# Splitting the last group of a decoder's last three layers into two sets of two batches

## The chip, the core and the metric

The kernel runs on one core of a Trainium2 chip. The metric is device microseconds of one execution. The profiler records one execution; all times inside the kernel come from that record, counted in microseconds from the start of its span. PE is the matrix engine, DVE the vector engine, ACT the scalar engine, POOL the general-purpose one, SP the engine that issues most DMAs.

## What is computed

A decoder of four blocks of three layers each runs over x, 32 batches of 128 tokens of width 128. Only the last block matters here:

```python
x = x + _L3_attn_ref(_layernorm(x), L3_attn_key_param, ...)   # layer 9
x = x + _L3_xattn_ref(_layernorm(x), ctx, ctx, mask, ...)     # layer 10
x = x + _L3_ffn_ref(_layernorm(x), weight_q, ...)             # layer 11
```

Layer 9 is an attention of 16 heads over 32 learned patterns whose weights are a sparsemax: the 32 scores of a token and head are sorted in descending order, the threshold tau is the largest of the means of the first k sorted scores less 1/k, and the weights are max(z - tau, 0). Layer 10 is a one-head attention over a context with a multiplicative mask. Layer 11 is a product with an integer weight: the normed row is scaled by its largest absolute value, clipped, rounded to whole numbers, multiplied, and scaled back.

## The kernel before

The 32 batches lie in 8 groups (G = 8) of 4 batches (J = 4); group i is the tile xg[i], 128 x 512 fp32. layer9() at its end writes out a schedule by hand for layers 9, 10 and 11 together. It is a loop over periods i = 0 to G + 2, each of 15 slots n = 0 to 14. In period i, slot n:

- sort(i, n) does step n of a merging sort of group i, for i below 8: two DVE tensor_tensor instructions (max and min) over up to 128 x 1024 elements each, and before them, where the step leaves elements untouched, two ACT copies of those. A step reads what the step before wrote, copies included.
- attend(i - 1) takes the sorted scores of the group before: slots 0 to 3 turn them over on PE, find tau, subtract it on POOL; slots 3 to 7 turn the weights over (turn_z), multiply with the values; slots 8 to 11 put the heads in order and project, and DVE adds the result to x.
- layer10(i - 2) does slots 0, 1, 2, 3, 5, 6, 7, and its first two steps (the norm) lie in slots 12 and 14 of the period before.
- scores(i + 1) makes the scores of the next group in slots 4, 6, 7, 8, 11, 12.
- layer11(i - 2) does slots 8, 10, 11, 12, 14 and its last step slot 0 of the next period.

follow(T, A, V) makes PE, ACT and DVE keep the order of this program while there are sorts; once slot == G * 15 the call follow() lifts that, and the tail (the attend, layer 10 and layer 11 of the last group) is ordered by the tool's own scheduler. POOL and SP are never held to it. In periods 0 to 2 pieces of layer 8 are mixed in.

Layer 11's rounding is a pair of tensor_scalar instructions on E, which is POOL but for the last group, where it is DVE (L2088 and L2089; adding and subtracting 1.5 * 2^23 leaves whole numbers). The second writes bf16. In slot 14 PE turns the bf16 tile over against a bf16 identity and ACT copies it out; in slot 0 of the next period PE multiplies with wq, DVE scales and adds (four scalar_tensor_tensor, one tensor_tensor) and SP sends x out (L2104).

```python
        E.tensor_scalar(q, q, 127.0, -128.0, ALU.min, ALU.max)      # L2088
        E.tensor_scalar(qb, q, rnd, rnd, ALU.add, ALU.subtract)     # L2089, qb is bf16
```

PSUM has three tags of two buffers each: ps (one bank a buffer), two and acc. Every turning over and most products take a ps; in layer 10 the tile of scores keeps one of the two ps buffers from slot 1, where it is written, to slot 3, where the last exp reads it.

SP's loads of context and mask for layer 10 (L325, L2027) are written in slot 12, but SP is not held to the program's order, so they run ahead.

Nearly all DVE, ACT and PE rows carry line L192, the helper that records the order; rows are told apart by their tiles. bbig holds sorted scores, gbig scores (z) and the re-ordered heads, xn a normed x, s small columns.

Of the kernel before, what the change touches and what calls it, by code (L numbers as in the profile page):

```python
# [10 lines left out]
F32 = mybir.dt.float32  # L11
# [191 lines left out]
def program(ctx, tc, cols, x, ctxt, mask, drop, dfirst, dsmall, dwide, drows, dunits, dexperts, dconst, drel, dwq, out):  # L203
# [38 lines left out]

    def follow(*engines):

        for e in (V, A, T):
            e.keep(e in engines)
# [107 lines left out]
    def norm_act(src, o):  # L354

        st, mv, rs, sh = small(J, 6), small(J, 2), small(J), small(J)
        for j in range(J):
            V.bn_stats(st[:, j, :], src[:, j, :])
        for j in range(J):
            V.bn_aggr(mv[:, j, :], st[:, j, :])  # L360
        V.tensor_scalar(rs, mv[:, :, 1], EPS, None, ALU.add)
        P.tensor_tensor(rs, rs, K["nhalf"], ALU.pow)
        yield
        V.scalar_tensor_tensor(sh, mv[:, :, 0], -1.0, rs, ALU.mult, ALU.mult)
        for j in range(J):
            A.activation(o[:, j, :], src[:, j, :], AF.Identity, bias=sh[:, j : j + 1], scale=rs[:, j : j + 1])
        yield

    def layernorm_act(i):

        xn = mid.tile([128, J, D], F32, tag="xn", name="xn", bufs=2)
        steps = norm_act(xg[i], xn)
        next(steps)
        yield
        next(steps)
        xnT = mid.tile([128, 512], F32, tag="xnT", name="xnT", bufs=2)
        transposed(xn, xnT, A.copy)
        yield xnT
# [1457 lines left out]
    def layer9():  # L1836
# [16 lines left out]
        def scores(i):  # L1853

            steps = norm_turned(i, WW["L3_attn_bo"])
            next(steps)
            yield
            next(steps)
            yield
            xnT = next(steps)  # L1860
            yield
            qT = linearT(W["a3_Wq"], xnT, W["L3_attn_bq"])
            z = zs[i] = gbig((128, J, 512))
            yield
            for part in range(2):
                p = two()
                for j in range(2):
                    at = (2 * part + j) * 128
                    mm(p[:, j], qT[:, at : at + 128], flat(kb))
                A.mul(z[:, 2 * part : 2 * part + 2], p, 8**-0.5)  # L1870
                ordered[i] = flat(z)
                yield
# [4 lines left out]
        def sort(i, n):  # L1877

            p, d = steps[n]
            cur, nxt = ordered[i], bbig()  # L1880
            ordered[i] = nxt
            a, b = (t.rearrange("p (n k) -> p n k", k=2 * p) for t in (cur, nxt))
            if d < p:
                A.copy(b[:, :, 0:d], a[:, :, 0:d])
                A.copy(b[:, :, 2 * p - d :], a[:, :, 2 * p - d :])
                a, b = (t[:, :, d : 2 * p - d] for t in (a, b))
            lo, hi, lo2, hi2 = (
                bass.AP(t.tensor, t.offset + at, [list(t.ap[0]), list(t.ap[1]), [2 * d, max(p // d - 1, 1)], [1, d]])
                for t in (a, b) for at in (0, d))
            V.tensor_tensor(lo2, lo, hi, ALU.max)  # L1890
            V.tensor_tensor(hi2, lo, hi, ALU.min)

        def attend(i):

            z, top, sTs, aTs = zs[i], ordered[i], {}, {}

            def turn_top(c):
                t = ps()
                for j in range(J):
                    T.transpose(t[:, j * 128 : (j + 1) * 128], top[:, j * 512 + c * 128 : j * 512 + c * 128 + 128], ident)  # L1900
                sTs[c] = bmid()
                A.activation(sTs[c], t, AF.Identity, bias=K["minus"])

            def lower(c):
                tau, m, sT = small(J, 4), acc((128, J, 4, 32)), sTs.pop(c)
                for j in range(J):
                    mm(m[:, j].rearrange("p h k -> p (h k)"), sT[:, j * 128 : (j + 1) * 128], K["means"])
                V.tensor_reduce(tau, m, AX.X, ALU.max)
                part = z[:, :, c * 128 : c * 128 + 128].rearrange("p j (h k) -> p j h k", k=32)
                P.tensor_tensor(part, part, bc(tau, 3, 32), ALU.subtract)  # L1910

            def turn_z(c):
                t = ps()
                for j in range(J):
                    T.transpose(t[:, j * 128 : (j + 1) * 128], z[:, j, c * 128 : (c + 1) * 128], ident)
                aTs[c] = bmid()
                A.activation(aTs[c], t, AF.Relu)
# [17 lines left out]
            yT_ps = acc()  # L1935
# [5 lines left out]
            yT = gmid()  # L1941
# [4 lines left out]
            rows = gbig((32, 16, 16, 8))  # L1946
            for c in range(0, 4, 2):
                t = two((32, 8, 128))
                for n in range(8):
                    T.transpose(t[:, n, :], by[:, 4 * c + n, :], ident)  # L1950
                A.copy(rows[:, :, 4 * c : 4 * c + 8, :], t.rearrange("p l (h e) -> p h l e", h=16))
                yield
            t = ps((128, 16, J, 8))
            for h in range(16):
                T.transpose(t[:, h].rearrange("p j l -> p (j l)"), rows[:, h].rearrange("p l e -> p (l e)"), ident[0:32, 0:32])
            yT = gmid((128, J, 16, 8))
            for j in range(J):
                A.copy(yT[:, j], t[:, :, j])
            yield
            zs.pop(i), ordered.pop(i)  # L1960
            project(i, yT.rearrange("p j h l -> p (j h l)"), W["a3_Wo"], None)
# [18 lines left out]
        for i in range(G + 3):  # L1980
            for n in range(15):
                todo = []
                add = lambda f, g, *at: todo.extend((f, g) for a in at if a == n and 0 <= g < G)
                add(layer11, i - 3, 0)
                add(attend, i - 1, 0, 1, 2, 3, 4, 5, 6, 7, 8, 9, 10, 11)
                add(layer10, i - 2, 0, 1, 2, 3, 5, 6, 7)
                add(layer10, i - 1, 12, 14)
                add(scores, i + 1, 4, 6, 7, 8, 11, 12)
                add(layer11, i - 2, 8, 10, 11, 12, 14)
                schedule.append((i, n, todo))  # L1990
        follow(T, A, V)
        for slot, (i, n, todo) in enumerate(schedule):
            if slot == G * 15:
                follow()
# [4 lines left out]
            if i < G:  # L1999
                sort(i, n)  # L2000
# [8 lines left out]

    def norm_turned(i, bo):  # L2010

        xn, xnT = (mid.tile(shape, F32, tag=tag, name=tag, bufs=2) for shape, tag in (([128, J, D], "xn"), ([128, 512], "xnT")))
        steps = norm_act(xg[i], xn)
        next(steps)
        yield
        next(steps)
        P.tensor_tensor(xg[i], xg[i], bc(bo, 1, J), ALU.add)
        yield
        transposed(xn, xnT, A.copy)
        yield xnT  # L2020


    def layer10(i):

        E = P if i < G - 1 else V
        c, dm = load_ctx(i), gmid((128, J, D))
        SY.dma_start(out=dm, in_=drop[i * J : i * J + J].rearrange("b q k -> q b k"))  # L2027
# [7 lines left out]
        s = ps((128, J, 128))  # L2035
        for j in range(J):
            cols_j = slice(j * 128, (j + 1) * 128)
            mm(s[:, j, :], xnT[:, cols_j], ctxT[i][:, cols_j])
        m, den, rec = small(J), small(J), small(J)
        pr = bmid((128, J, 128))  # L2040
# [3 lines left out]
        for half in range(2):  # L2044
            for j in (2 * half, 2 * half + 1):
# [5 lines left out]
        prT = bmid()  # L2051
        transposed(pr, prT, A.copy)
        yield
        o = ps()
        for j in range(J):
            cols_j = slice(j * 128, (j + 1) * 128)
            mm(o[:, cols_j], c[:, j, :], prT[:, cols_j])
        yT = gmid()
        A.copy(yT, o)
        yield  # L2060
        p = ps((128, J, 128))
        for j in range(J):
            mm(p[:, j, :], yT[:, j * 128 : (j + 1) * 128], W["x3_W"])
        for j in range(J):
            V.scalar_tensor_tensor(xg[i][:, j, :], p[:, j, :], rec[:, j : j + 1], xg[i][:, j, :], ALU.mult, ALU.add)
# [3 lines left out]
    def layer11(i):  # L2069

        rnd = 1.5 * 2.0**23
        E = P if i < G - 1 else V
        xn = mid.tile([128, J, D], F32, tag="xn", name="xn", bufs=2)
        steps = norm_act(xg[i], xn)
# [3 lines left out]
        P.tensor_tensor(xg[i], xg[i], bc(WW["qbias"], 1, J), ALU.add)  # L2078
        yield
        am, inv = small(J), small(J)  # L2080
# [4 lines left out]
        q, qb = bmid((128, J, D)), gmid((128, J, D), BF16)  # L2085
        for j in range(J):
            A.mul(q[:, j, :], xn[:, j, :], inv[:, j : j + 1])
        E.tensor_scalar(q, q, 127.0, -128.0, ALU.min, ALU.max)  # L2088
        E.tensor_scalar(qb, q, rnd, rnd, ALU.add, ALU.subtract)  # L2089
        yield  # L2090
        t = ps((128, 512), BF16)
        for j in range(J):
            T.transpose(t[:, j * 128 : (j + 1) * 128], qb[:, j, :], identb)
        qT = gmid((128, 512), BF16)
        A.copy(qT, t)
        yield
        p = ps((128, J, 128))
        o = bmid((128, J, D))
        for j in range(J):
            mm(p[:, j, :], qT[:, j * 128 : (j + 1) * 128], wq)  # L2100
        for j in range(J):
            V.scalar_tensor_tensor(o[:, j, :], p[:, j, :], am[:, j : j + 1], WW["qscale"], ALU.mult, ALU.mult)
        V.tensor_tensor(xg[i], xg[i], o, ALU.add)
        SY.dma_start(out=out[i * J : i * J + J].rearrange("b s d -> s b d"), in_=xg[i])  # L2104
# [53 lines left out]
```

## Time and profile before

| | us |
|---|---|
| median of 3 runs | 2979.89 (2970.95 to 2987.02) |
| the profiled execution | 2967.81, span 2965.9 |
| busy in the span: PE, DVE, ACT, POOL | 2552.0, 2072.2, 1504.4, 972.2 |
| the sorts' max and min, bbig from bbig, from 2400 us on | 237.4 in 224 instructions |
| L2089 (POOL, writes bf16) | 1.93 to 2.72, 7 times |
| L2104, x out: from issue to landing | 2.4 |

The periods can be read in the trace by the sort's first step, which reads gbig: it starts at 2758.5, 2806.3 and 2854.05. A full period is 47.75 us long; the last, with group 7's sort, 44.6 (to 2898.66); the tail 67.2. A row of the timeline gives start, duration, engine, line, operation, output and inputs, shapes, how many instructions were merged into it and, in brackets, how long the engine had been idle and what ended that. A row of the windows gives each engine's busy time and, after them, the granted clock of PE as a share of full speed.

### The profile page before, as it was taken

To read this page: it belongs to the slowest core of one execution; us is meant where nothing else is said; L and a number is where in the kernel's file an instruction comes from. 1 tells how busy PE (TensorE), PEld (TensorE's weight loads), DVE (VectorE), ACT (ScalarE), POOL (GpSimd) and SP (SyncE) were. 2 spreads that over 40 slices of the span, in tenths; PEclk is the share of its full clock that TensorE was granted. 3 is DMA by queue.
4 is the path that set the end of the run, shared out by engine and by line. 5 is a ranking of instruction groups with operands and counts; after the bars stand their busy time and mean duration, and the time that the engine had idled before them with its cause. 6 is when DMAs were issued, how large, how long until landed. Compare 5 with 4: busy or idle time off the path is not lost.

```text
span 2965.9 us, 55573 instructions
## 1 busy us (share of the span) xinstructions
PE 2552.0 (86%) x22609; PEld 1641.3 (55%) x22628; DVE 2072.2 (70%) x4121; ACT 1504.4 (51%) x3360; POOL 972.2 (33%) x1009
## 2 busy tenths in 40 slices
PE   6889999999889989999998999987886977976664
PEld 3555667777644446566664444445554666644443
DVE  6877667878878756677786544458886415789893
ACT  4555545444412256666664444457773323456663
POOL 4443342223210123334551000124442365324432
PEclk8877789999999999999999999989997998998786
DMA  3000000000000010000000000000002255210000
GB/s 113 2 2 2 6 20 8 5 8 1 12 11 1 0 33 2 5 9 9 12 2 15 1 1 0 1 1 2 2 2 82 94 179 166 91 29 12 22 11 18
DMA packets 50464, 73.44 MB, mean 25 GB/s; under 512 B 3841, under 2 KB 40962, under 8 KB 50082
## 3 DMA queue, kind: packets, MB, share of 16 engines
q1 hardware_dynamic: 41968, 33.05, 3.7%
q0 software_dynamic: 7808, 33.71, 3.5%
q8 instruction: 178, 2.92, 0.4%
q10 hardware_dynamic: 434, 3.14, 0.3%
q14 instruction: 76, 0.62, 0.1%
HBM read 57.00 MB, written 12.89 MB: 24 GB/s over the span
## 4 chain that ended last, share of the span: by engine, by line
PE 52%; DVE 29%; ACT 7%; POOL 7%; issue 3%; DMA 2%; DVEq 0%; ACTq 0%; POOLq 0%; SPq 0%
PE ps L192 21%; PE two L192 17%; PE acc L192 14%; DVE bbig L192 12%; DVE s L192 9%; DVE bmid L192 3%; DVE gmid L192 3%; ACT bbig L192 3%; POOL xn L399 3%; ACT bmid L192 1%; ACT xn L192 1%; POOL s L397 1%; DVE x L192 1%; ACT gmid L192 1%; DMA we<-in_experts,wrow 1%
## 5 line engine op out<-in xcount | busy, mean ns | idle before, releaser
L192 PE MATMUL ps<-cs,bbig 128*128 128x128 f32 x2208 | 330.3, 290 | 83.4 <-ACT bbig L192 34.6
L192 PEld LDWEIGHTS ps<-cs,bbig 128*128 128x128 f32 x2208 | 254.8, 147 | 187.3 <-ACT bbig L192 84.0
L192 ACT COPY bbig<-ps 128x512 f32<-128x512 f32 x418 | 229.2, 591 | 241.5 <-PE ps L192 241.4
L192 DVE TENSOR_REDUCE s<-two 128x8 f32<-128x1024 f32 (+1 forms) x192 | 234.1, 1220 | 119.6 <-PE two L192 118.4
L192 PE MATMUL two<-xnT,u 128*128 128x512 f32 x512 | 262.4, 613 | 11.8 <-ACT bmid L192 6.3
L192 DVE TENSOR_TENSOR bbig<-bbig 128x1024 f32<-128x1024 f32 (+3 forms) x234 | 249.6, 1108 | 7.3 <-ACT bbig L192 5.8
L192 PE MATMUL acc<-bmid,u 128*128 128x512 f32 x416 | 221.3, 619 | 20.1 <-DVE bmid L192 18.8
L192 PE MATMUL two<-gbig,gmid 32*128 32x512 f32 (+1 forms) x1248 | 216.5, 567 | 2.4 <-ACT bbig L192 2.4
L192 DVE TENSOR_TENSOR bmid<-bmid,ps 128x512 f32<-128x512 f32 x192 | 130.0, 684 | 114.8 <-ACT bmid L192 94.7
L479 POOL TENSOR_SCALAR gbig<-bmid,cs 128x512 f32<-128x512 f32 x96 | 148.7, 1565 | 162.8 <-ACT bmid L192 162.8
L192 ACT ACTIVATE bbig<-two,s 128x256 f32<-128x256 f32 (+1 forms) x512 | 189.7, 419 | 20.8 <-DVE s L192 17.4
L192 ACT ACTIVATE bbig<-bbig 128x512 f32<-128x512 f32 (+1 forms) x160 | 128.1, 801 | 87.1 <-DVE bbig L192 86.6
L192 PEld LDWEIGHTS two<-xnT,u 128*128 128x128 f32 x512 | 92.8, 193 | 116.4 <-issue 56.5
L192 ACT ACTIVATE bmid<-two 128x512 f32<-128x512 f32 x88 | 52.5, 597 | 183.3 <-PE two L192 175.0
L192 ACT ACTIVATE bmid<-two,ws 128x512 f32<-128x512 f32 x128 | 85.1, 686 | 115.1 <-PE two L192 115.0
L192 PEld LDWEIGHTS acc<-bmid,u 128*128 128x128 f32 x416 | 76.7, 197 | 115.1 <-DVE bmid L192 60.8
L192 ACT ACTIVATE bbig<-bbig,s 128x128 f32<-128x128 f32 x384 | 118.7, 388 | 29.0 <-DVE s L192 29.0
L1068 POOL TENSOR_TENSOR bbig<-bbig,s 128x1024 f32<-128x1024 f32 x32 | 60.6, 1893 | 214.2 <-PE two L192 152.7
L192 DVE TENSOR_TENSOR bbig<-two,s 128x1024 f32<-128x1024 f32 (+1 forms) x128 | 122.6, 958 | 9.0 <-ACT bbig L192 0.5
L491 POOL MEMSET val<- 128x512 f32 x72 | 39.5, 551 | 259.1 <-PE acc L192 258.1
L192 PE MATMUL ps<-cs,xn 128*128 128x128 f32 x288 | 66.5, 320 | 65.3 <-ACT xn L192 36.9
L192 PE MATMUL two<-xT,we 128*128 128x128 f32 (+1 forms) x576 | 102.5, 333 | 18.8 <-DMA we<-in_experts,wrow 14.8
(313 smaller groups left out, 5914.2 us busy)
## 6 DMA issues: line engine op xcount, KB each, us to landing
u<-in_units SPq DMA_DIRECT2D x10, 768.0 KB, 4.3
gmid<-in_ctx SPq DMA_DIRECT2D x16, 256.0 KB, 3.0
x<-in_x SPq DMA_DIRECT2D x8, 256.0 KB, 9.1
gmid<-in_mask SPq DMA_DIRECT2D x8, 256.0 KB, 3.1
ys<-bbig SPq DMA_DIRECT2D x2, 1024.0 KB, 6.6
gmid<-ys SPq DMA_DIRECT2D x8, 256.0 KB, 4.0
gmid<-in_drop SPq DMA_DIRECT2D x8, 256.0 KB, 3.4
out<-x SPq DMA_DIRECT2D x8, 256.0 KB, 2.4
```

The costliest lines, as they stand in the source:

```text
L192: d = f(*args, **kwargs)
L397: P.tensor_tensor(rs, rs, K["nhalf"], ALU.pow)
L399: P.tensor_scalar(xn[:, j, :], xg[i][:, j, :], mv[:, j, 0:1], rs[:, j : j + 1], ALU.subtract, ALU.mult)
L479: P.tensor_scalar(o[:, n, :], k, K["n4"][:, n : n + 1], None, ALU.mult)
L491: P.memset(o, 0.0)
L1068: (V if c2 else P).tensor_tensor(pr[:, four, :], pr[:, four, :], bc(nm[:, four], 2, 256), ALU.mult)
```

## The change

The schedule runs over nine sets rather than eight groups: groups 0 to 6 as before, and group 7 as two sets of two batches. Each has its own sort (half as wide, the same 15 steps), attend, layer 10 and layer 11. The schedule has 12 periods rather than 11, and the order is lifted after nine. Every function takes the number of batches n from the set; norm_act takes it as an argument. Sets 7 and 8 (g = 7) round on DVE.

Layer 11's rounding stays in fp32, in place; PE turns over the fp32 tile in slot 0 of the next period, ACT writes bf16 as it copies it out of PSUM, and the last step moves from slot 0 to slot 2. layernorm_act, which nothing calls, goes.

```diff
+    sets = [(i, xg[i], J) for i in range(G - 1)] + [(G - 1, xg[G - 1][:, j : j + 2], 2) for j in (0, 2)]
+    def few(n, *shape):
+        return small(J, *shape)[:, 0:n]
+    def turn_set(t, o, n):
+        p = ps((128, n * 128))
+        for j in range(n):
+            turn_over(p[:, j * 128 : (j + 1) * 128], t[:, j, :])
+        A.copy(o, p)
+        return o
...
         def sort(i, n):
-            cur, nxt = ordered[i], bbig()
+            cur, nxt = ordered[i], bbig((128, sets[i][2] * 512))
...
-        for i in range(G + 3):
+        for i in range(len(sets) + 3):
...
-                add(layer11, i - 3, 0)
+                add(layer11, i - 3, 0, 2)
...
-                add(layer11, i - 2, 8, 10, 11, 12, 14)
+                add(layer11, i - 2, 8, 10, 11, 12)
...
-            if slot == G * 15:
+            if slot == len(sets) * 15:
                 follow()
...
-            if i < G:
+            if i < len(sets):
                 sort(i, n)
...
         def layer11(i):
-        q, qb = bmid((128, J, D)), gmid((128, J, D), BF16)
+        q = bmid((128, n, D))
...
-        E.tensor_scalar(qb, q, rnd, rnd, ALU.add, ALU.subtract)
+        E.tensor_scalar(q, q, rnd, rnd, ALU.add, ALU.subtract)
         yield
-        t = ps((128, 512), BF16)
-        for j in range(J):
-            T.transpose(t[:, j * 128 : (j + 1) * 128], qb[:, j, :], identb)
-        qT = gmid((128, 512), BF16)
-        A.copy(qT, t)
+        qT = turn_set(q, gmid((128, n * 128), BF16), n)
         yield
...
-        SY.dma_start(out=out[i * J : i * J + J].rearrange("b s d -> s b d"), in_=xg[i])
+        first = g * J + 2 * (i - g)
+        SY.dma_start(out=out[first : first + n].rearrange("b s d -> s b d"), in_=x)
```

The rest of the diff replaces J by n, and xg[i] by the set's x, in scores, attend, norm_turned, layer10 and layer11; layer 10 loads the context and the mask of its own set's batches.

## The prediction

> **What bounds the kernel now.** I read the page first: it says that the span is 2965.9 us and that DVE is busy over 80% in the last fifth, but it mixes twelve layers. So I cut the end of the span at the first sort step of each period (windows):
>
> ```profile
> core 0: us, PE busy (x) PEld busy (x) DVE busy (x) ACT busy (x) POOL busy (x), PEclk, DMA share, GB/s
> 2806.30:2854.05 47.75, 33.20 (x166) 21.73 (x166) 43.01 (x81) 29.88 (x67) 20.42 (x14) 0.82 0.06 17
> 2854.05:2898.66 44.61, 24.54 (x156) 18.20 (x156) 42.26 (x72) 25.52 (x59) 17.09 (x12) 0.77 0.07 18
> 2898.66:2928.03 29.37, 22.35 (x148) 17.40 (x148) 9.43 (x30) 14.97 (x35) 8.92 (x8) 0.85 0.10 28
> 2928.03:2950.16 22.13, 9.42 (x40) 7.47 (x40) 6.17 (x26) 6.76 (x20) 4.80 (x4) 0.50 0.04 12
> 2950.16:2965.90 15.74, 1.22 (x8) 0.69 (x8) 5.60 (x20) 3.51 (x9) 2.29 (x2) 0.50 0.05 17
> ```
>
> The first two rows are a full period and group 7's: DVE is busy 90 and 95% of them, so DVE bounds. The next three are the tail, 67.2 us: group 7's attend, its layer 10, its layer 11. No engine is half busy in the last two; one instruction waits for the next, and PE's granted clock is down at 0.50. The tail is what the split can shorten; the periods are what it lengthens.
>
> The timeline across a period's border shows what the layer 11 edit touches:
>
> ```profile
> 2803.53 2.77 DVE L192 TENSOR_TENSOR bbig<-bbig 128x960 f32<-128x960 f32 x2 [0.77 <-ACT bbig L192]
> 2803.89 2.72 POOL L2089 TENSOR_SCALAR gmid<-bmid 128x512 bf16<-128x512 f32 x1
> ...
> 2806.30 2.35 DVE L192 TENSOR_TENSOR bbig<-gbig 128x1024 f32<-128x1024 f32 x2
> ...
> 2806.66 0.61 PE L192 MATMUL ps<-identb,gmid 128*128 128x128 bf16 x4 [5.78 <-POOL gmid L2089]
> ...
> 2809.22 1.13 DVE L192 SCALAR_TENSOR_TENSOR bmid<-ps,s,ww 128x128 f32<-128x128 f32 x4 [0.58 <-PE ps L192]
> ```
>
> PE sits 5.78 us behind POOL's bf16 write and then keeps DVE 0.58 us. And while POOL writes, the sort step beside it takes 2.77 us; in group 7's period, where L2089 ended before that step, steps 13 and 14 together took 4.42, of which step 13 is 2.10 elsewhere, so step 14 is 2.32.
>
> **The layer 11 edit, five full periods (3 to 7).** Removed on the path: 2.77 - 2.32 = 0.45 us of DVE time, if POOL's second instruction is as short in fp32 as the first, and the 0.58 us wait. POOL's price in fp32 is not in the trace: the nearest row below is L2088, the same shape into fp32, 0.61; above, L2089 itself, 1.93 undisturbed. [...] I take 0.61, as L2088 also has two operations; at 1.93 the 0.45 goes. Added: PE turns fp32 instead of bf16. A warm group of four takes 0.60 either way (2814.30 and 2806.66), a slow-clock one 1.11 against 0.61, hidden in slot 0 by the sort's 2.35.
>
> Moved: DVE's 1.13 + 0.69 goes from slot 0 to slot 2, and a ps buffer with it. In slot 2 layer 10's scores hold one of the two ps buffers, so the last turning over of sorted scores (turn_top(3)) now waits until DVE has read layer 11's product, after the sort step. Queued behind it: on PE the last lower product, on ACT its copy, then the exps and the copies of sort step 4. I laid this out with the durations of the trace. Before, turn_top(3) starts 10.4 us into the period and sort step 4 at 15.86. After: slot 0 and 1 sorts end at 4.7; ACT, still held to 1.76 by layer 10's xn, copies qT, two tops and xnT to 4.3; the lower products run from 3.6, 2.3 us earlier; sort step 2 starts at 8.1 rather than 10.34 and ends at 10.1; four scalings to 11.25; turn_top(3) 11.3, ACT copy to 12.5, the exps to 15.5, sort step 4 at 15.8. So the 2.2 us gained are spent on the 1.8 moved and on ACT: net -0.05. At worst DVE waits for ACT's copies, +1.0 us a period; at best the 0.58 and the earlier tops come through whole, -1. SP sends x some 7 us later, ahead of the loads of context and mask; those now go out in slot 0 of the period before their use (2811.6 for use after 2854), so 7 us of 40 is free. Sum: five times (-0.45 - 0.05) = -2.5 us, bounds -7 and +5.
>
> **The split, sorts.** A pair of 1024 elements takes 2.35, a pair of 512 (2830.51) 1.29: two halves cost 0.23 more than a whole. Fifteen steps: +3.5 us of DVE; the pairs of the full period add up to 31.9, so a half is 17.7. [...]
>
> **The split, group by group.** Period 7 (set 7, half a sort) still holds the four-batch attend(6), layer10(5), layer11(5), and half a scores. Attend(6)'s own pace decides. From the period's start to its addition to x (2843.33 in the full period) it takes 37.0 us beside a full sort; in the tail, without sort, 28.8 (2898.5 to 2927.34). Beside half a sort I take the middle, 32.9. Behind that, DVE alone: addition 0.69, abs-max 0.68, two small 0.35, step 12 half 0.95, a norm 1.4, steps 13 and 14 half 1.07 and 1.14: 6.3. Period 7 = 39.2 against 44.6: of 14 us of sort taken away only 5.4 are saved, since ACT's copies, PE and POOL are then what each slot waits for.
>
> Period 8 (set 8) holds half an attend, but layer10(6) and layer11(6) whole. Layer 10 adds to x 25.4 us into the period before and 21.7 in the tail; with half an attend beside it I lay 18.2 (the slot 2 sort at 6.8, exps done 11.7, three products with copies to 18.1). Four additions 1.05, half step 8 0.95, norm 1.35, POOL's power 1.0 to 1.8 under half steps 9 and 10, then ACT's xn 1.65, abs-max and scale 1.05: 27.0; half steps 12 to 14 and half a norm 4.2: 31.2. DVE's own work there is some 24 us, the lower bound.
>
> Tail, set 8 alone. Most rows halve above a fixed part (ACT 512 elements 0.59, taken as 0.37 for 256; DVE 0.69 to 0.36; PE products half), but POOL's power (1.03), the two 32 x 1024 copies (1.0 each, now 16 rows of the same length) and the DMA's end (3.6) don't. Attend: 16.9 against 28.8. Layers 10 and 11, link by link: addition and first norm to xn 3.7, turn and copy 1.0, scores 1.1, max to exps 1.5, mask 0.5, turn and copy 1.0, two products with the copy between 2.7, scaling 0.6, norm 3.3, quantising 2.6, turn, copy, product 1.4, end 4.6: 24.0 against 38.6. With 0.7 for set 7's layers beside it: 41.6 against 67.2.
>
> Sum: 39.2 + 31.2 + 41.6 = 112.0 against 44.6 + 67.2 = 111.8: +0.2. The extra period costs what the shorter tail saves. With -2.5 from layer 11: -2.3 us on the profiled 2967.81, of which 1.9 lie outside the span: 2965.5. The median of the runs is 12.1 above that execution, for no reason in the program, so the forecast stands on the median: 2979.9 - 2.3 = 2977.6.
>
> **Rivals.** *A, the wash (0.62):* 2977.6. Its own range comes from the layer 11 bounds (-7 to +5) and 4 us either way on three stages: 2968 to 2987. For it: every gain and loss is read from a stage. Against: my chains leave out short waits.
>
> *B, the half periods don't shrink (0.18), slower.* The program's order on DVE, ACT and PE makes every slot wait for attend and copies; with four queues in lockstep a half period could take the pace of group 7's, 44.6. Then 89.2 + 41.6 - 111.8 = +19.0, and with -2.5: 2996.4. It turns slower than 0.5% when the two together reach 89 us rather than 70.4. For it: period 7's saving is already only 5.4 us by my sum, and in the ordinary period DVE waits for ACT's copies in steps 13 and 14. Against: in the tail, where nothing of the sort stands between, the same attend takes 28.8.
>
> *C, the order of layer 11 was dearer than its row (0.13), faster.* If the tops' earlier start comes through and POOL's release takes its other slowed steps, too, 2 us in each of five periods instead of 0.5 give -10, and with a tail of 37 instead of 41.6 (the free scheduler fills it better) -4.6, and +0.2: -14.4, 2965.5.
>
> *D, it doesn't do what it says (0.07):* the tail's order is the scheduler's, and set 7's layers could be put ahead of set 8's, so that the tail shortens only to some 47 us: 5.4 + 0.2 - 2.5 = +3.1, 2983.
>
> About 0.5% (15 us) is what a measurement of this kernel can tell from no change. From the cases: faster 0.13, same 0.70, slower 0.17. The range 2962 to 2995 takes in A, D, most of C and the lower half of B.
>
> **What would show it.** Right: periods 3 to 6 within 1 us of 47.75 and L2089 near 0.6; two half periods of some 39 and 31; a tail near 41; DVE below 80% busy in them. Wrong: half periods above 44 (B); full periods below 46 (C), or above 48.5 with DVE waiting for ACT at sort step 4 (slot 2's buffer); a PE wait for POOL that stays.

## The result and the profile after

The changed kernel takes 3005.89 us (median of 7 runs, 2992.71 to 3013.62) against 2981.46 for the kernel before (7 runs, 2970.95 to 2988.73): the ratio is 1.0075, interval 1.0054 to 1.0097. The two medians lie some 24 us apart, where 2.3 us less had been forecast; 3005.89 lies above the forecast's range. The profiled execution took 2992.71, with a span of 2990.9.

Up to the start of period 3 the two traces are level (2661.4 and 2662.0 us). So the difference of these two executions lies behind it. The windows of the changed kernel, cut as before: periods 3 to 6 together, period 7 and 8 (sets 7 and 8), set 8's attend in the tail, the rest of the tail.

```profile
core 0: us, PE busy (x) PEld busy (x) DVE busy (x) ACT busy (x) POOL busy (x), PEclk, DMA share, GB/s
2662.03:2864.24 202.21, 136.51 (x661) 90.87 (x659) 186.18 (x329) 117.64 (x264) 76.20 (x52) 0.77 0.06 16
2864.24:2908.18 43.94, 31.95 (x158) 21.77 (x157) 31.07 (x79) 23.99 (x64) 14.53 (x13) 0.73 0.07 19
2908.18:2943.40 35.22, 20.18 (x116) 14.31 (x116) 29.07 (x68) 19.62 (x57) 12.17 (x12) 0.69 0.06 16
2943.40:2967.20 23.80, 17.19 (x100) 12.55 (x100) 7.09 (x26) 10.45 (x27) 5.86 (x8) 0.79 0.08 23
2967.20:2990.90 23.70, 7.15 (x24) 4.33 (x24) 7.40 (x31) 5.00 (x15) 2.86 (x4) 0.50 0.04 12
```

The four full periods took 192.7 us before (2661.36 to 2854.05) and take 202.2: +9.5. There the split changes one thing only: period 6 makes the scores of set 7, half as many. Their mean granted PE clock fell from 0.82 to 0.77. What follows them takes 126.7 instead of 111.9: +14.9. And the tail did shrink, from 67.2 to 47.5, its last part, layers 10 and 11 of set 8, to the forecast 24.

Where a full period loses most of its time is seen on PE, from the product for the third tau on. First the timeline of before, period 6, then of the changed kernel, period 6:

```profile
2815.68 1.16 PE L192 MATMUL acc<-cs,bmid 128*128 128x128 f32 x8
2816.67 0.60 PE L192 MATMUL ps<-cs,bbig 128*128 128x128 f32 x4
2818.34 1.16 PE L192 MATMUL acc<-cs,bmid 128*128 128x128 f32 x8 [1.06 <-ACT bmid L192]
2819.33 0.60 PE L192 MATMUL ps<-cs,gbig 128*128 128x128 f32 x4
2820.68 1.05 PE L192 MATMUL acc<-bmid,vb 128*32 128x512 f32 x2 [0.75 <-ACT bmid L192]
```

```profile
2822.43 0.38 PE L192 MATMUL ps<-wq,gmid 128*128 128x128 bf16 x4
2822.64 1.11 PE L192 MATMUL acc<-cs,bmid 128*128 128x128 f32 x8
2826.53 0.66 PE L192 MATMUL ps<-cs,bbig 128*128 128x128 f32 x4 [2.78 <-DVE bmid L192]
2828.03 2.08 PE L192 MATMUL acc<-cs,bmid 128*128 128x128 f32 x8 [0.84 <-ACT bmid L192]
2829.90 1.06 PE L192 MATMUL ps<-cs,gbig 128*128 128x128 f32 x4
2831.70 1.91 PE L192 MATMUL acc<-bmid,vb 128*32 128x512 f32 x2 [0.75 <-ACT bmid L192]
```

The row ps<-cs,bbig is turn_top(3). Before, it follows the product without a gap; now layer 11's product (ps<-wq,gmid) has the only free ps buffer, and PE stands 2.78 us until DVE has read it. The prediction had this wait. It did not have what comes behind it: the same eight products take 2.08 us instead of 1.16, the turnings-over 1.06 instead of 0.60, two of the value products (weights with values) 1.91 instead of 1.05. The windows from turn_top(3) to the start of the last value products show why; first before, then changed:

```profile
2816.65:2827.84 11.19, 8.38 (x49) 4.80 (x47) 11.16 (x21) 8.09 (x20) 8.01 (x4) 1.00 0.00 0
```

```profile
2826.50:2842.40 15.90, 13.60 (x46) 7.14 (x46) 14.83 (x20) 7.25 (x18) 6.17 (x4) 0.57 0.18 49
```

The value behind POOL's is the granted clock: 1.00 before, 0.57 now. The chain of attend, which goes PE, ACT, PE, ACT through these slots, is stretched from 11.2 to 15.9 us.

A smaller loss lies ahead of that wait. The first 16 products for tau now run earlier in the period, most of them at half the clock (0.50 up to 6.4 us into period 6); first before, then changed:

```profile
2812.17 2.29 PE L192 MATMUL acc<-cs,bmid 128*128 128x128 f32 x16
```

```profile
2816.45 3.32 DVE L192 TENSOR_TENSOR bbig<-bbig 128x1024 f32<-128x1024 f32 x2
2818.11 3.10 PE L192 MATMUL acc<-cs,bmid 128*128 128x128 f32 x16
2820.06 0.69 DVE L192 TENSOR_REDUCE s<-acc 128x16 f32<-128x512 f32 x1 [0.30 <-PE acc L192]
```

Sort step 1, the row at 2816.45, is slower too: 3.32 us instead of 2.35, beside POOL's addition of a bias (2815.91 to 2817.55). That costs nothing here, since DVE still waits 0.30 us for PE behind it.

POOL's second rounding instruction, now in fp32, is no faster than it was:

```profile
L2101 POOL TENSOR_SCALAR bmid<-bmid x7: 1927/2712/2725, 2658.6 to 2941.7; 128x512 f32<-128x512 f32 x7
```

Shortest, median and longest in ns: before they were 1927, 2714 and 2722, writing bf16.

### The profile page after: what moved, and what is told of

The parts are those of the page before. It is cut to its first block, busy times and chain, and to the rows that moved or that the text cites. A ratio compares the mean times of both kernels' runs of the same rounds, so it can differ in the third digit from the quotient of the medians.

```text
span 2990.9 us, 55768 instructions
## 1 busy us (share of the span) xinstructions
PE 2558.3 (86%) x22651; PEld 1641.9 (55%) x22670; DVE 2093.3 (70%) x4172; ACT 1509.0 (50%) x3397; POOL 966.6 (32%) x1019
## 4 chain that ended last, share of the span: by engine, by line
PE 52%; DVE 30%; ACT 7%; POOL 6%; issue 3%; DMA 2%; another core or an unknown queue 0%; DVEq 0%; ACTq 0%; POOLq 0%; SPq 0%
PE ps L192 20%; PE two L192 17%; PE acc L192 15%; DVE bbig L192 11%; DVE s L192 10%; DVE bmid L192 4%; DVE gmid L192 3%; POOL xn L391 3%; ACT bbig L192 3%; ACT bmid L192 2%; DVE x L192 1%; POOL s L389 1%; ACT gmid L192 1%; DMA we<-in_experts,wrow 1%; ACT xn L192 1%
## 5 line engine op out<-in xcount | busy, mean ns | idle before, releaser
L192 DVE TENSOR_TENSOR bbig<-bbig 128x512 f32<-128x512 f32 (+8 forms) x262 | 264.2, 1049 | 5.1 <-ACT bbig L192 3.0
L192 ACT ACTIVATE bbig<-two,s 128x256 f32<-128x256 f32 (+1 forms) x512 | 189.7, 419 | 20.3 <-DVE s L192 16.9
L483 POOL MEMSET val<- 128x512 f32 x72 | 38.5, 537 | 262.2 <-PE acc L192 261.1
L192 DVE TENSOR_TENSOR h<-h,two 128x512 f32<-128x512 f32 x66 | 45.3, 686 | 103.6 <-ACT h L192 87.5
```

The costliest lines, as they stand in the source:

```text
L192: d = f(*args, **kwargs)
L483: P.memset(o, 0.0)
```

## The experiments

*Theory 1, buffer and clock:* layer 11's last step in slot 2 makes PE wait, PE's granted clock drops behind the wait, and the slow products cost the time; the split by itself costs little. *Theory 2, lockstep:* the half periods don't shrink because each slot waits for the next engine; layer 11 costs only the 9.5 us of the full periods.

In this table the times are of one profiled execution each, in us. The ratio (with its 95% interval) is that of all runs, 7 to 22 of a kernel, to those of the kernel before on the same chip. The last column is the mean of the eight value products' durations in periods 3, 4, 5 and 6, in ns; at a granted clock of 1.00 (before, period 6) they take 604. A drop that ends before these products, as in periods 3 and 4 of the changed kernel, doesn't show there.

| kernel | periods 3 to 6 | periods with group 7's sorts | tail | period 3 to the end | ratio | value products |
|---|---|---|---|---|---|---|
| before | 192.7 | 44.6 | 67.2 | 304.5 | 1 | 604 604 604 605 |
| changed | 202.2 | 43.9, 35.2 | 47.5 | 328.9 | 1.0075 (1.0054 to 1.0097) | 605 605 911 947 |
| split_only | 192.3 | 38.5, 32.9 | 45.2 | 308.9 | 1.0032 (1.0011 to 1.0054) | 698 604 605 604 |
| layer11_only | 204.9 | 47.0 | 65.8 | 317.7 | 1.0044 (1.0022 to 1.0065) | 878 947 947 947 |
| product_in_two | 191.2 | 38.3, 37.0 | 45.3 | 311.8 | 1.0036 (1.0016 to 1.0057) | 809 715 601 601 |
| clock_fill | 191.3 | 41.1, 34.9 | 47.6 | 314.9 | 1.0075 (1.0046 to 1.0104) | 604 604 604 604 |
| layer11_fill | 192.5 | 45.9 | 66.3 | 304.7 | 1.0007 (0.9987 to 1.0027) | 604 604 604 604 |
| last_step_slot4 | 191.7 | 39.0, 31.8 | 46.6 | 309.1 | 1.0016 (0.9995 to 1.0037) | 779 604 604 604 |
| fp32_old_slots | 192.2 | 44.3 | 68.2 | 304.7 | 1.0011 (0.9990 to 1.0033) | 698 604 604 604 |
| warm_two_places | 196.6 | 45.5 | 66.0 | 308.1 | 1.0022 (1.0003 to 1.0042) | 605 832 604 832 |
| wait_alone | 202.7 | 46.4 | 67.5 | 316.6 | 1.0046 (1.0023 to 1.0068) | 604 605 929 947 |
| layer11_slot4 | 192.3 | 44.0 | 66.5 | 302.7 | 1.0005 (0.9990 to 1.0019) | 784 604 604 604 |

Single executions of one edited kernel lie up to 1.4% apart, and the longer ones mostly have the lower mean granted clock over the span: split_only's runs went from 2960.5 us at 0.926 to 3003.2 at 0.907. In the traces much of the scatter lies ahead of the part that was edited: period 3 starts anywhere from 2650.7 us (layer11_slot4) to 2685.1 (layer11_only). So totals are compared by the ratio, and the traces are read for what happens in a period.

**split_only**, the two halves of the change apart:

```diff
-                add(layer11, i - 3, 0, 2)
+                add(layer11, i - 3, 0)
...
-                add(layer11, i - 2, 8, 10, 11, 12)
+                add(layer11, i - 2, 8, 10, 11, 12, 14)
```

with the bf16 rounding and turning over of before.

> Layer 11 as before (bf16 rounding, turned over in slot 14, last step in slot 0), the nine sets kept. Theory 1 (buffer and clock): nearly all of the loss comes from layer 11's last step in slot 2, which takes the free ps buffer, makes PE wait 2.8 us for DVE and drops its granted clock from 1.00 to 0.57 in slots 3 to 6. Then full periods are back at 47.75, the half periods take some 40 and 32 and the tail 44: a span of some 2970, ratio to before 1.001. Theory 2 (lockstep): half periods don't shrink because every slot waits for the next engine in the program's order; they stay near 43.9 and 35.2 and the tail at 47.5: a span of some 2981, ratio 1.005.

The half periods do shrink, to 38.5 and 32.9; with the tail, 116.6 against 111.9 before. Theory 2 falls. The split is a loss of its own, though, of 4.7 us in this part of the trace and 0.32% by the ratio, more than the 0.1% expected. Its windows (periods 7, 8, attend of set 8, the rest):

```profile
2854.80:2893.30 38.50, 26.73 (x160) 18.68 (x160) 30.72 (x78) 23.95 (x64) 14.87 (x14) 0.85 0.08 22
2893.30:2926.20 32.90, 17.79 (x116) 13.52 (x116) 27.47 (x68) 19.61 (x57) 12.46 (x12) 0.76 0.06 17
2926.20:2948.10 21.90, 15.35 (x100) 11.26 (x100) 7.55 (x27) 10.67 (x27) 5.56 (x8) 0.81 0.09 25
2948.10:2971.40 23.30, 6.80 (x24) 3.97 (x24) 7.61 (x32) 5.12 (x15) 3.02 (x4) 0.50 0.04 12
```

Against the forecast 39.2, 31.2, 16.9 (plus 0.7) and 24.0, the third is where it is: set 8's attend takes 21.9.

**layer11_only**, the other half:

```diff
-    sets = [(i, xg[i], J) for i in range(G - 1)] + [(G - 1, xg[G - 1][:, j : j + 2], 2) for j in (0, 2)]
+    sets = [(i, xg[i], J) for i in range(G)]
```

> The layer 11 edit alone, eight groups of four batches. Theory 1: the four full periods cost +9.5 as in the changed kernel, group 7's period some +2.5, the tail +1: a span of 2979, ratio 1.0044; with split_only's small cost the two add up to less than the whole, since the half periods suffer from the slot 2 wait as well. Theory 2: only the +9.5 of the full periods, ratio 1.0033, and the two parts add up to the whole +25.

+13.2 in the trace, 12.2 of it in the four full periods, and 1.0044: the layer 11 edit, which touches a few instructions a period, is by these medians the larger half. In the changed kernel the same periods cost 9.5; its period 6, with half as many scores to make, takes 50.2 us against 51.2 here. By the ratios the two parts add up to the whole (0.32 and 0.44 to 0.75%); by the traces 4.4 and 13.2 make 17.6 of 24.4. The rest fits the half periods, which have the same wait (1.8 us in period 7 and 2.3 in period 8, and a drop to 0.50 behind each).

**product_in_two**, the wait taken away by another buffer, in the changed kernel:

```diff
-        p = ps((128, n, 128))
+        p = two((128, n, 128))
         o = bmid((128, n, D))
```

> The changed kernel with one word edited: layer 11's last product goes to a buffer of the tag two, which is idle in slot 2, instead of ps. Nothing else moves. Theory 1: the wait of PE for DVE before turn_top(3) goes, the granted clock in slots 3 to 6 is back at 1.00, full periods take 47.0 to 47.8, the half periods some 40 and 32: a span of some 2970, ratio to before 1.001. Theory 2: full periods return but the half periods stay near 43 and 35, ratio 1.005.

turn_top(3) starts 2.6 to 3.2 us earlier in periods 4 to 6 (8.9 to 9.3 us into the period, against 11.5 to 12.5), the full periods fall from 202.2 to 191.2, below those of before, and the ratio from 1.0075 to 1.0036. That is next to split_only's 1.0032 and above the 1.001 expected. What is left is not all as in split_only: period 8 takes 37.0 us against 32.9, at a granted clock of 0.68 against 0.76. This wasn't followed up.

**clock_fill**, the wait kept and filled with work, in the changed kernel:

```diff
             lower(2)
+            fill = two((128, 8, 128))
+            for k in range(24):
+                T.transpose(fill[:, k % 8, :], ident, ident)
             turn_top(3)
```

> The changed kernel with 24 more turnings-over of the identity on PE, into a buffer that nobody reads, between the third lower product and turn_top(3): PE's wait for DVE is filled with work instead of taken away. Theory 1: turn_top(3) starts as late as in the changed kernel, but the granted clock stays at 1.00 in slots 3 to 6, the value products take 1.05 instead of 1.91, and the full periods take 47.8 to 48.6: most of the 2.5 us a period comes back although work was added. If the wait itself is the cost and not the clock, the periods stay at 50.2 or grow.

In the trace just that: turn_top(3) is as late in periods 4 to 6 (11.6 to 12.3), the value products take 604 ns, the full periods 191.3 rather than 202.2. But the ratio, from nine runs, is still 1.0075 (1.0046 to 1.0104). The profiled run was the fastest of the nine, so the trace may not stand for the others. By the ratio this run speaks against theory 1, and it stays unexplained; the next repeats it without the split.

**layer11_fill**, the same lines in layer11_only:

> The layer 11 edit alone on eight groups, with the 24 turnings-over of the identity in slot 2 that keep PE at work through its wait. Theory 1 (the wait costs by the clock that it loses): the value products take 605 ns instead of 947, the four full periods 46 to 47 us instead of 51, and the ratio to before falls from layer11_only's 1.0044 to 0.998 to 1.001. If the clock is not the cost (or is lost elsewhere instead), the periods stay near 51 and the ratio at 1.0044 or above, since work was added.

With 24 more instructions a period the ratio falls from 1.0044 to 1.0007, and the two intervals overlap only between 1.0022 and 1.0027; the four periods fall from 204.9 to 192.5. All of that is in periods 4 to 6 (46.4, 46.7 and 47.1, before 47.5, 47.7 and 47.8). In period 3, where the added work doesn't fill the wait (2.4 us are left), it is 52.3 against 49.7 before. The timelines of PE, period 6, first layer11_only, then layer11_fill:

```profile
2851.47 0.66 PE L192 MATMUL ps<-cs,bbig 128*128 128x128 f32 x4 [2.80 <-DVE bmid L192]
2852.97 2.08 PE L192 MATMUL acc<-cs,bmid 128*128 128x128 f32 x8 [0.84 <-ACT bmid L192]
2854.84 1.06 PE L192 MATMUL ps<-cs,gbig 128*128 128x128 f32 x4
2856.64 1.91 PE L192 MATMUL acc<-bmid,vb 128*32 128x512 f32 x2 [0.75 <-ACT bmid L192]
```

```profile
2831.82 2.46 PE L192 MATMUL two<-cs 128*128 128x128 f32 x21
2834.51 0.66 PE L192 MATMUL ps<-cs,bbig 128*128 128x128 f32 x4 [0.23 <-DVE bmid L192]
2836.00 1.16 PE L192 MATMUL acc<-cs,bmid 128*128 128x128 f32 x8 [0.84 <-ACT bmid L192]
2836.99 0.60 PE L192 MATMUL ps<-cs,gbig 128*128 128x128 f32 x4
2838.34 1.04 PE L192 MATMUL acc<-bmid,vb 128*32 128x512 f32 x2 [0.75 <-ACT bmid L192]
```

The row two<-cs is the added work (21 of its 24 products are in this view); turn_top(3) still waits for DVE behind it. The rows after it run at full clock (1.00 from 2835.5 to 2847.0). So in periods 4 to 6 the cost was the lost clock, not the lost 2.8 us.

**last_step_slot4**, the step moved on instead:

```diff
-                add(layer11, i - 3, 0, 2)
+                add(layer11, i - 3, 0, 4)
```

> The changed kernel with layer 11's last step in slot 4 instead of slot 2, when the exps have given back the second ps buffer. Theory 1 (one free ps buffer in slot 2): turn_top(3) no longer waits for DVE, but the same wait can come back at turn_z in slots 4 and 5, shorter since two buffers rotate: full periods 47.5 to 49, halves 41 and 34, span some 2976, ratio 1.003 to 1.004, like product_in_two. If not the buffer but the moved DVE work is the cost: full periods stay at 50, ratio 1.0075.

1.0016 in place of 1.0075; the full periods 191.7. The same work on DVE two slots later doesn't hold PE up: turn_top(3) starts 7.9 to 8.5 us into periods 4 to 6, without a wait. By then the scores have given their ps buffer back.

**fp32_old_slots**, the fp32 rounding and turning over alone, on eight groups, in the slots of before (the two add lines of split_only in layer11_only):

> Eight groups, layer 11 with the fp32 rounding and the fp32 turning over, but in the slots of before (turned over in slot 14, last step in slot 0). Theory 1: the rounding is not the cost; POOL's second instruction takes its 1.93 to 2.72 us in fp32 as well, so nothing is gained either: full periods 47.7 to 48.3, ratio 1.000 to 1.001. A third theory (fp32 turning over, 1.11 instead of 0.61 us on PE ahead of the sorted scores, is what delays the period): full periods 49 or more, ratio 1.003.

1.0011, no difference that can be told, and at most 0.33%: neither the rounding nor the fp32 turning over is the main cost, and nothing is gained on POOL.

**warm_two_places**, layer11_fill with the same kind of work in slot 14 too:

```diff
             for key in todo:
                 go(key)
+            if n == 14 and 3 <= i < len(sets):
+                fill = two((128, 8, 128))
+                for k in range(48):
+                    T.transpose(fill[:, k % 8, :], ident, ident)
```

> layer11_fill with 48 more turnings-over of the identity in slot 14 of each period from 3 on, where PE waits 5.8 us for POOL and its granted clock is at 0.50 in the following 5 us. If the clock is what counts: slots 0 and 1 run at 1.00, sort step 2 starts 1 to 2 us earlier, full periods 45 to 46.5, ratio 0.995 to 0.999, a version that beats both kernels. If DVE bounds the period by then: nothing more than layer11_fill, or up to 1 us a period lost where the added work holds PE up.

A miss: 1.0022, which can't be told from layer11_fill's 1.0007, and in periods 4 and 6 the clock dropped after all (832 ns). There PE still waits 1.10 us before turn_top(3); in period 5, which kept its clock, it waits 0.26. More work in another slot didn't hold the clock where it is needed; why these two periods differ from period 5 wasn't tried.

**wait_alone**, the kernel before with the wait and nothing else of the change:

```diff
+            if i >= 2:
+                held = ps((128, 128))
+                T.transpose(held, ident, ident)
+                V.tensor_copy(acausal[:, 0:1], held[:, 0:1])
             lower(2)
             turn_top(3)
```

> The kernel before, with nothing of the change, but with a ps buffer taken in slot 2 of the attends of groups 2 to 7: PE turns the identity over into it and DVE reads one column of it behind sort step 2. That is the wait of the changed kernel without its moved work (some 0.6 us of PE and 0.2 us of DVE added). Theory 1: turn_top(3) starts when DVE is through, PE stands some 2 us, the granted clock drops in slots 3 to 6 (value products 850 to 950 ns in most periods), the full periods take 49 to 51, ratio 1.002 to 1.005. If the 1.8 us of DVE work that the change moved into slot 2 were the cost: full periods within 0.5 of 47.75, ratio 1.000 to 1.001.

It is slower by 0.46% (0.23 to 0.68). PE in its period 6:

```profile
2829.39 0.66 PE L192 MATMUL ps<-cs,bbig 128*128 128x128 f32 x4 [1.91 <-DVE acausal L192]
2830.89 2.07 PE L192 MATMUL acc<-cs,bmid 128*128 128x128 f32 x8 [0.84 <-ACT bmid L192]
2832.75 1.06 PE L192 MATMUL ps<-cs,gbig 128*128 128x128 f32 x4
2834.56 1.91 PE L192 MATMUL acc<-bmid,vb 128*32 128x512 f32 x2 [0.75 <-ACT bmid L192]
```

A buffer that waits some 2 us for an instruction that reads a single column does as much harm (0.46%) as the whole layer 11 edit (0.44%). DVE is no busier for it: 43.4 us of this period of 51.1, against 43.0 of 47.75 before.

**layer11_slot4**, last_step_slot4 without the split:

> Eight groups, the layer 11 edit with its last step in slot 4: last_step_slot4 without the split. Theory 1: the split costs some 5 us by itself (split_only), so without it the four full periods stay at 191.7 and group 7 and the tail return to 112: from the start of period 3 to the end 303 to 304 against 304.5, ratio 0.998 to 1.001; if anything beats the kernel before, it is this one. If the split is no loss once the wait is gone: the same ratio as last_step_slot4, 1.0016.

1.0005 (0.9990 to 1.0019), a tie with the kernel before: the loss of the layer 11 edit is gone. From last_step_slot4 (1.0016) the ratio alone doesn't tell it apart. No version was found that beats the kernel before.

## Why the prediction was wrong

**The step that failed** is the working of the layer 11 edit, slots 0 to 4: "net -0.05", "at worst [...] +1.0 us a period". It named the buffer, the wait, and the queue behind it, and then used for that queue the durations that the rows have in the trace of before, where PE's longest wait in slots 2 to 6 of period 6 is 1.06 us. Measured in period 6: sort step 2 starts at 9.3 us rather than 8.1, turn_top(3) at 12.5 rather than 11.3, sort step 4 at 18.4 rather than 15.8. The cost of period 6 is +2.4 instead of -0.5, and layer11_only, which has no split to help, has +3.1 a period (+12.2 over four). layer11_fill and wait_alone show that the main missing term is the clock behind the wait: with it kept, periods 4 to 6 come to 0.7 to 1.1 us less than before.

The 1.2 us by which sort step 2 and turn_top(3) are late have been lost by then, and to the clock as well: the first 16 products for tau start 4.0 us into the period rather than 3.6, and moved into the slow start of the period they take 3.10 us instead of 2.29.

The trace of before had both clocks in it: 1.00 in slots 3 to 6, and 0.50 in the tail from 2928.03 on, where the same eight products take 2.08 us instead of 1.06:

```profile
2814.74 1.06 PE L192 MATMUL ps<-ctxT,xnT 128*128 128x128 f32 x8
2936.83 2.08 PE L192 MATMUL ps<-ctxT,xnT 128*128 128x128 f32 x8 [0.68 <-ACT xnT L192]
```

The prediction priced the slow one where that trace showed it, in slot 0 and in the tail, and not where the change would put idle time, in slot 2. In period 6 of wait_alone a shorter wait, of 1.91 us with 0.84 more right behind, came with the slow clock too: eight products took 2.07 us instead of 1.16.

One price was read at the wrong clock: the bf16 group at 2806.66, which the prediction calls warm, took its 0.61 us at 0.50 (2806.30 to 2809.72). At 0.99 (2820.47 to 2824.00 of the changed kernel) four bf16 products of that shape take 0.38 us, and four turnings-over in fp32 0.60.

The value products' column makes this look like chance, but every such wait in periods 3 to 6 of the changed kernel (5.01, 3.32, 2.77 and 2.78 us) came with a drop to 0.50, in the wait or right behind it. In wait_alone periods 4 and 5 show the same drop, and period 6 a mean of 0.61 from 2829.0 to 2846.5. What differs is its length. The slow stretches of periods 4 and 5, first of the changed kernel, then of wait_alone:

```profile
2724.94:2731.76 6.82, 4.04 (x16) 3.24 (x16) 6.29 (x10) 1.88 (x7) 1.96 (x1) 0.50 0.41 115
2776.13:2789.79 13.66, 11.39 (x34) 5.50 (x31) 12.47 (x21) 6.67 (x17) 6.50 (x4) 0.50 0.21 59
```

```profile
2731.28:2734.69 3.41, 2.87 (x12) 2.53 (x12) 2.55 (x3) 1.19 (x5) 2.76 (x1) 0.50 0.00 0
2779.07:2792.72 13.65, 11.38 (x32) 5.36 (x30) 11.10 (x21) 6.68 (x17) 7.22 (x4) 0.50 0.00 1
```

In period 4 of both kernels the stretch is over before the value products start. What decides its length wasn't tried.

**POOL in fp32**, taken as 0.61, lies at the other end of its bounds: 1.93 to 2.73. So the 0.45 us of relief for DVE was never there. Writing bf16 is not what makes it slow, since writing fp32 takes as long (2.71 us in the median, as before). L2100 (minimum, maximum) takes 0.61 in the median on the same shape and also has two operations, so that count, from which the prediction took its 0.61, did not tell the price; what makes the second pair slow, its operations or something else, wasn't tried.

**The split.** Expected +0.2, measured +4.7 in split_only. Period 7 (39.2 forecast, 38.5), period 8 (31.2, 32.9) and layers 10 and 11 in the tail (24.0, 23.3) were near. Set 8's attend was forecast 4.3 too short (17.6 with its surcharge, 21.9). Its first tops queue on PE behind group 6's layer 11, whose rounding on POOL ends 0.8 us after the last sort, and start 2.5 us after it. In the tail of before they start 2.7 us after it, so this part did not halve. The other 1.8 us weren't traced. The sum also left out a gain: period 6, with half the scores to make, takes 45.3 us in split_only and 47.8 before. So the mechanism held and the size didn't.

**The half periods at 43.9 and 35.2** look like rival B, but split_only shows that they shrink when the wait is not there: B's mechanism isn't the cause. Rival C had the sign wrong. Rival D's number for the tail, some 47, came out in the changed kernel (47.5), but its reason is not shown: in split_only, with a tail of 45.2, what stands ahead of set 8's first tops is group 6's layer 11, not set 7's layers. The claim that DVE bounds the full periods held only as long as the attend chain had slack; wait_alone, where DVE has no more to do and idles longer, shows that chain taking over.

## What to carry over

When an edit makes PE wait, price not only the wait but the instructions behind it at PE's slow rate, where an idle stretch of the same trace shows one: here the tail of before, with eight products in 2.08 us instead of 1.06. Price a moved row at the clock of the place that it moves to: the first 16 products for tau took 3.10 us there instead of 2.29. A PSUM buffer is a queue, and here PE stood 2.78 us in it: before moving a step to another slot, list who holds each buffer there and until when. And halving the work of a stage that is a chain of small steps can save far less than half: the attend in the tail went from 28.8 to 21.9 us.

## What the runs showed of the hardware

Adding work made a kernel faster: 24 matrix instructions a period that nobody reads took the ratio from 1.0044 (layer11_only) to 1.0007 (layer11_fill). The same lines in the changed kernel left the ratio at 1.0075 (clock_fill), which stays open. The wait put into wait_alone, 1.91 us of PE in its period 6, came with slow stretches at a granted clock of 0.50, 3.41 us long in period 4 and 13.65 in period 5. The whole kernel's time went with the mean granted clock, 2960.5 us at 0.926 and 3003.2 at 0.907 in split_only. On POOL one tensor_scalar of 128 x 512 takes 0.61 us in the median and the next, of the same shape and type, 1.93 to 2.73 (changed kernel). And a sort step on DVE that took 2.35 us before took 3.32 in the changed kernel, beside a POOL instruction of 1.64.
